# Reciprocal roots of the norms by Newton steps on VectorE, and the normalised input written by one VectorE product

## The chip, the core and the metric

The program runs on one core of a Trainium2 chip. The core has a matrix engine (TensorE, PE in the profile), a vector engine (VectorE, DVE), a scalar engine with function tables (ScalarE, ACT), a general engine (GpSimd, POOL) and a queue engine (SyncE, SP). Each works through its own list of instructions in order; an instruction starts when those before it on its engine have gone and the semaphores it waits for have been raised. The metric is the device time of one execution in microseconds (us): the median of several runs.

## What is computed

The input is one sequence of 2048 tokens with 256 features. Six sublayers follow one another. Each takes a layer norm of `x` first and adds its result to `x`:

```python
x = x + 0.5 * L0_ffn(layernorm(x))     # stage f0
x = x + L0_attn(layernorm(x))          # attention of layer 0
x = x + 0.5 * L0_ffn(layernorm(x))     # stage f1
x = x + 0.5 * L1_ffn(layernorm(x))     # stage f2
x = x + L1_attn(layernorm(x))          # attention of layer 1
x = x + 0.5 * L1_ffn(layernorm(x))     # stage f3

def _layernorm(x, axis=-1, eps=1e-05):
    m = jnp.mean(x, axis=axis, keepdims=True)
    v = jnp.var(x, axis=axis, keepdims=True)
    return (x - m) / jnp.sqrt(v + eps)

def rms_norm(x):
    inv = jax.lax.rsqrt(jnp.mean(xf * xf, axis=-1, keepdims=True) + eps)
    return (xf * inv).astype(x.dtype)
```

The feed-forward of layer 0 quantises its weights to three values per group of 64, computes `silu(gate) * up` over 1024 hidden features, takes an RMS norm of that, and projects back. The feed-forward of layer 1 keeps the two largest of each four hidden values. Attention has 16 heads of 16 features, a causal mask and, in layer 0, a linear position bias; layer 1 has a rotary embedding and biases.

## The kernel before

**Layout.** Everything is held with features on the partitions and tokens along the free axis. The 2048 tokens are cut into `NCH` = 4 chunks of `CH` = 512. `xs[c]` is the residual of chunk c, `xns[c]` its normalised form, each a tile of 128 partitions by 2 by 512 (`DC` = 2 halves of the features). The order on all four compute engines is the order of the program text (a manual schedule): what the generators below emit first runs first on its engine.

**A layer norm** is the generator `layernorm(c, name)`, lines 242 to 273, whose pieces are emitted between other work. GpSimd adds the two halves (line 249); TensorE multiplies by a matrix of 1/256 (line 253), which leaves the mean on every partition; VectorE subtracts it (line 255, tile `xc`); ScalarE squares (line 258); GpSimd adds the halves (line 260); TensorE takes the mean again (line 264). Then `root` (lines 202 to 209) transposes blocks of 32 by 32 on VectorE (line 206) so that the 512 variances stand as 128 by 16 values, and takes `Sqrt` on ScalarE (line 208). In the next piece `spread` (lines 211 to 219) takes the reciprocal on VectorE (line 213) and transposes back with a broadcast (line 215) into `sd`, 128 by 512. Last, GpSimd multiplies `xc` by `sd`, once for each half (line 269):

```python
nc.vector.transpose(tt.rearrange("p b s -> p (b s)"), ps)               # L206
nc.scalar.activation(r, tt[:, :, 0], AF.Sqrt, bias=eps, scale=scale)    # L208
nc.vector.reciprocal(r, r)                                              # L213
nc.gpsimd.tensor_tensor(xn[:, dc, :], xc[:, dc, :], sd, ALU.mult)       # L269
```

There are 24 layer norms. The RMS norm of layer 0's feed-forward uses the same `root` and `spread` in `tail0` (lines 349 to 371), 8 times, so `root` runs 32 times. The RMS result multiplies the projection on VectorE (line 369).

**ScalarE's tables.** `Silu` (line 317), `Exp` (lines 753 and 756) and `Sqrt` (line 208) need different function tables; the profile shows a table load ahead of the first instruction of another function, charged to that instruction's line.

**Feed-forward stages** (`feed_forwards`, lines 435 to 487) walk over chunks and, in each, over 8 blocks of 128 hidden features (f = 0 to 7). A step emits the matmuls of gate and up into one of two pairs of PSUM banks (line 306 in layer 0, 12 matmuls in bf16; line 281 in layer 1, 4 in f32), the `Silu` on ScalarE (line 317) and the product on VectorE (line 318). In layer 0 two more VectorE instructions split the product into bf16 parts (lines 334 and 329), and ScalarE and GpSimd build the sum of squares (lines 339, 340 and 336). In layer 1 `sparsify` (lines 385 to 421) compares and selects with VectorE (lines 394, 412 to 414, 418) and GpSimd (lines 405 to 409). After each step `pull()` (line 191) emits the next piece of up to two waiting layer norms, and the tail of the chunk before (`tail0` or `tail1`) emits one of its pieces. Stage f0 also quantises the weights on VectorE (lines 158 to 170). `split` (lines 234 to 240) divides `xns[c]` into bf16 parts on VectorE ahead of a chunk of layer 0.

**Attention** (`attention`, line 490) first finds the maxima of the scores: TensorE writes scores (lines 671 and 679) into one of three PSUM banks, VectorE reduces them (line 682). Transposed scores (lines 733, 741) then go through `Exp` on ScalarE (line 753) and into the product with the values (line 768). VectorE turns and divides the result (lines 789, 793, and on GpSimd 794). `prep_qk` makes the keys and queries of the next chunk (lines 536 to 588; in layer 1 GpSimd works at line 575).

**Where the layer norms fall.** By the times of line 206, 10 roots fall in stage f0 (three at its start, at 15, 61 and 63 us), 3 in the first attention (271, 289 and 382 us), 8 in f1, 5 in f2, 3 in the second attention (1240, 1256 and 1364 us) and 3 in f3 (two together at 1788 us).

Of the kernel before, what the change touches and what calls it, by code (L numbers as in the profile page):

```python
# [11 lines left out]

F32 = mybir.dt.float32
BF16 = mybir.dt.bfloat16
AF = mybir.ActivationFunctionType
ALU = mybir.AluOpType
AX = mybir.AxisListType
# [2 lines left out]
P = 128  # L20
S = 2048
E = 256
DC = E // P
H = 16
D = E // H
SLOT = 32
# [3 lines left out]
CH = 512  # L30
# [16 lines left out]
def macaron_kernel(ctx: ExitStack, tc: tile.TileContext, a, out):  # L47
    nc = tc.nc

    cpool = ctx.enter_context(tc.tile_pool(name="const", bufs=1))  # L50
# [10 lines left out]
    def ps_one(name):  # L61
        return ps3.tile([P, CH], F32, tag="one", name=name)
# [26 lines left out]
    make_identity(nc, ident)  # L89
    ident_b = cpool.tile([P, P], BF16, name="ident_b")  # L90
    nc.vector.tensor_copy(ident_b, ident)

    mask_qk = cpool.tile([P, P], BF16, name="mask_qk")
    mask_kq = cpool.tile([P, P], BF16, name="mask_kq")
    for mask, step, row in ((mask_qk, -1, 1), (mask_kq, 1, -1)):
# [5 lines left out]

    half_m = cpool.tile([P, P], BF16, name="half_m")
    nc.vector.memset(half_m, 0.0)
# [4 lines left out]
    nc.vector.memset(mean_m, 1.0 / E)  # L108
    ones_m = cpool.tile([P, P], F32, name="ones_m")
    nc.vector.memset(ones_m, 1.0)  # L110
    eps_ln = cpool.tile([P, 1], F32, name="eps_ln")
    nc.vector.memset(eps_ln, 1e-5)
    eps_rms = cpool.tile([P, 1], F32, name="eps_rms")
    nc.vector.memset(eps_rms, 4 * float(np.finfo(np.float32).eps))


    lpool = ctx.enter_context(tc.tile_pool(name="ln", bufs=1))
# [4 lines left out]
    w0pool = ffn0_scope.enter_context(tc.tile_pool(name="weights0", bufs=1, side="right"))  # L122
    wgu0 = w0pool.tile([P, DC, 2 * F], BF16, name="wgu0")
    wp0 = w0pool.tile([P, FC, E], BF16, name="wp0")
    raw_scope = ExitStack()
# [3 lines left out]
    def quantize(i):  # L129
# [19 lines left out]
        aw = qp.tile([P, 512], BF16, tag="aw", bufs=4, name=f"aw{i}")  # L149
        nc.scalar.activation(aw, raw, AF.Abs)  # L150
        sg = qp.tile([P, 512], BF16, tag="sg", bufs=4, name=f"sg{i}")
        nc.scalar.activation(sg, raw, AF.Sign)
        yield
# [48 lines left out]
    def root(ps, eps, scale, name):  # L202


        tt = lpool.tile([P, CH // SLOT, SLOT], F32, tag="tt", name=f"tt_{name}")
        nc.vector.transpose(tt.rearrange("p b s -> p (b s)"), ps)  # L206
        r = lpool.tile([P, CH // SLOT], F32, tag="r", bufs=3, name=f"r_{name}")
        nc.scalar.activation(r, tt[:, :, 0], AF.Sqrt, bias=eps, scale=scale)  # L208
        return r

    def spread(r, pool, bufs, name):

        nc.vector.reciprocal(r, r)  # L213
        sd = pool.tile([P, CH], F32, tag="sd", bufs=bufs, name=f"sd_{name}")
        nc.vector.transpose(
            sd.rearrange("p (b s) -> p b s", s=SLOT),
            r.unsqueeze(2).to_broadcast([P, CH // SLOT, SLOT]),
        )
        return sd
# [22 lines left out]
    def layernorm(c, name):  # L242

        pending[c] += 1

        def pieces():
            x, xn = xs[c], xns[c]
            s = lpool.tile([P, CH], F32, tag="s", bufs=2, name=f"s_{name}")
            nc.gpsimd.tensor_tensor(s, x[:, 0, :], x[:, 1, :], ALU.add)
            yield  # L250
            yield
            pm = ps_one(f"pm_{name}")
            nc.tensor.matmul(pm, lhsT=mean_m, rhs=s, start=True, stop=True)
            xc = lpool.tile([P, DC, CH], F32, tag="xc", bufs=2, name=f"xc_{name}")
            nc.vector.tensor_tensor(
                xc, x, pm.unsqueeze(1).to_broadcast([P, DC, CH]), ALU.subtract
            )
            nc.scalar.activation(xn, xc, AF.Square)
            v = lpool.tile([P, CH], F32, tag="s", bufs=2, name=f"v_{name}")
            nc.gpsimd.tensor_tensor(v, xn[:, 0, :], xn[:, 1, :], ALU.add)  # L260
            yield
            yield
            pv = ps_one(f"pv_{name}")
            nc.tensor.matmul(pv, lhsT=mean_m, rhs=v, start=True, stop=True)
            r = root(pv, eps_ln, 1.0, f"ln_{name}")
            yield
            sd = spread(r, lpool, 2, f"ln_{name}")
            for dc in range(DC):
                nc.gpsimd.tensor_tensor(xn[:, dc, :], xc[:, dc, :], sd, ALU.mult)  # L269
            pending[c] -= 1  # L270
            yield

        return pieces()


# [39 lines left out]
    def member(pg, to, hp, name):  # L315
        sl = hp.tile([P, CH], F32, tag="sl", bufs=2, name=f"sl_{name}")
        nc.scalar.activation(sl, pg[:, 0, :], AF.Silu)  # L317
        nc.vector.tensor_tensor(to, sl, pg[:, 1, :], ALU.mult)  # L318

    def steps0(c, xp, h, hp, own, name):  # L320
# [10 lines left out]
        for f in range(FC):  # L331
# [5 lines left out]
            else:  # L337
                sq = own.tile([P, CH], F32, tag="sq", bufs=2, name=f"sq_{name}_{f}")
                nc.scalar.activation(sq, h[:, f, :], AF.Square)  # L339
                nc.gpsimd.tensor_tensor(ss, ss, sq, ALU.add)  # L340
# [8 lines left out]
    def tail0(c, ss, parts, hp, name):  # L349

        yield
        pss = ps_one(f"pss_{name}")
        nc.tensor.matmul(pss, lhsT=ones_m, rhs=ss, start=True, stop=True)
        r = root(pss, eps_rms, 4.0 / F, f"rms_{name}")
        yield
        inv = spread(r, hp, 1, f"rms_{name}")
        for dc in range(DC):
            po = ps_one(f"po_{name}_{dc}")
            for f in range(FC):
                for part in range(3):  # L360
                    nc.tensor.matmul(
                        po,
                        lhsT=wp0[:, f, dc * P : (dc + 1) * P],
                        rhs=parts[f][part],
                        start=f == 0 and part == 0,
                        stop=f == FC - 1 and part == 2,
                    )
            y = hp.tile([P, CH], F32, tag="y", bufs=1, name=f"y_{name}_{dc}")
            nc.vector.tensor_tensor(y, po, inv, ALU.mult)
            nc.gpsimd.tensor_tensor(xs[c][:, dc, :], y, xs[c][:, dc, :], ALU.add)  # L370
            yield
# [793 lines left out]
```

## Time and profile before

| what | value |
|---|---|
| median of three runs | 1952.77 us (1952.13 to 1952.84) |
| the profiled execution, its own time | 1957.69 us |
| its span, first to last instruction | 1955.7 us |
| mean granted TensorE clock in it | 0.96 |
| table loads on ScalarE | 62, of 1283 ns each |
| GpSimd's products of line 269 | 48, 67.3 us in all |
| roots on ScalarE, line 208 | 32, of about 322 ns each |
| reciprocals on VectorE, line 213 | 32, of about 238 ns each |

The profile is taken from one execution, so durations and places below are read in its own span. Its lines name the engine, the line of the kernel, the tiles, a count, the busy time, the mean of one instruction and the idle time in front of it with what ended it. An engine that is idle costs nothing by itself; it matters where its work is the one that others wait for.

### The profile page before, as it was taken

To read this page: it belongs to the slowest core of one execution; us is meant where nothing else is said; L and a number is where in the kernel's file an instruction comes from. 1 tells how busy PE (TensorE), PEld (TensorE's weight loads), DVE (VectorE), ACT (ScalarE), POOL (GpSimd) and SP (SyncE) were. 2 spreads that over 40 slices of the span, in tenths; PEclk is the share of its full clock that TensorE was granted. 3 is DMA by queue.
4 is the path that set the end of the run, shared out by engine and by line. 5 is a ranking of instruction groups with operands and counts; after the bars stand their busy time and mean duration, and the time that the engine had idled before them with its cause. 6 is when DMAs were issued, how large, how long until landed. Compare 5 with 4: busy or idle time off the path is not lost. (4 is left out here: it accounts for less than half of the span.)

```text
span 1955.7 us, 26994 instructions
## 1 busy us (share of the span) xinstructions
PE 1761.4 (90%) x10684; PEld 726.5 (37%) x10684; DVE 1361.6 (70%) x2384; ACT 894.2 (46%) x1112; POOL 458.4 (23%) x418
## 2 busy tenths in 40 slices
PE   5699789999999999789999876898999999998997
PEld 1233344433433333333444333433333333333443
DVE  7866377787788883666575655868877888825664
ACT  4343254555555668334422312445555656673220
POOL 3455321101000000455453432211111000003422
PEclk9799899999999999989999986999999999999999
DMA  4000252213211000200000115222122110000000
GB/s 129 1 1 33 82 148 83 73 54 102 62 45 46 28 28 2 73 1 0 1 11 0 54 61 158 82 73 92 52 69 86 43 43 26 18 1 0 11 11 22
DMA packets 50510, 93.10 MB, mean 48 GB/s; under 512 B 5424, under 2 KB 33072, under 8 KB 50128
## 3 DMA queue, kind: packets, MB, share of 16 engines
q1 hardware_dynamic: 49296, 89.28, 14.8%
q10 hardware_dynamic: 1088, 2.10, 0.3%
q8 instruction: 84, 1.38, 0.3%
q14 instruction: 42, 0.34, 0.1%
HBM read 59.51 MB, written 27.26 MB: 44 GB/s over the span
## 5 line engine op out<-in xcount | busy, mean ns | idle before, releaser
L682 DVE TENSOR_REDUCE mx<-pq 128x1 f32<-128x512 f32 (+3 forms) x1280 | 708.6, 603 | 158.5 <-PE pq L679 91.2
L753 ACT ACTIVATE pT<-pst 128x1024 f32<-128x1024 f32 (+3 forms) x614 | 542.6, 896 | 334.9 <-PE pst L733 196.8
L671 PE MATMUL pq<-k,q 105*128 105x512 bf16 (+7 forms) x1280 | 378.8, 353 | 74.7 <-DVE mx L682 52.3
L733 PE MATMUL pst<-q,k 99*128 99x512 bf16 (+7 forms) x1280 | 357.7, 354 | 5.1 <-ACT pT L753 4.2
L768 PE MATMUL pav<-pT,va 128*32 128x256 f32 (+1 forms) x4608 | 352.4, 382 | 5.2 <-DVE yt L789 5.0
L281 PE MATMUL pg_f<-xn,wgu 128*128 128x512 f32 x512 | 229.8, 602 | 11.5 <-DVE hr_f L318 11.5
L794 POOL TENSOR_TENSOR zt<-yt,rd 128x64 f32<-128x64 f32 x128 | 38.4, 300 | 795.2 <-DVE rd L793 795.1
L733 PEld LDWEIGHTS <-k 105*128 105x128 bf16 (+1 forms) x1280 | 101.5, 98 | 254.1 <-issue 218.4
L317 ACT ACTIVATE sl_f<-pg_f 128x512 f32<-128x512 f32 x128 | 76.0, 594 | 251.8 <-PE pg_f L281 175.0
L671 PEld LDWEIGHTS <-q 105*128 105x128 bf16 (+1 forms) x1280 | 124.5, 100 | 148.0 <-issue 44.3
L306 PE MATMUL pg_f<-xn,wgu 128*128 128x512 bf16 x512 | 156.2, 413 | 19.5 <-DVE wgu L170 6.8
L768 PEld LDWEIGHTS pav<-pT,va 128*32 128x32 f32 x4608 | 93.8, 108 | 208.7 <-issue 174.8
L281 PEld LDWEIGHTS pg_f<-xn,wgu 128*128 128x128 f32 x512 | 98.6, 193 | 136.9 <-issue 121.0
L306 PEld LDWEIGHTS <-wgu 128*128 128x128 bf16 x768 | 77.7, 101 | 166.9 <-issue 74.7
L292 PE MATMUL po_f<-h_f,wd 128*128 128x512 f32 x256 | 116.3, 608 | 17.3 <-DVE h_f L418 17.3
L340 POOL TENSOR_TENSOR ss_f<-ss_f,sq_f 128x512 f32<-128x512 f32 x56 | 91.1, 1628 | 111.5 <-ACT sq_f L339 111.3
L679 PE MATMUL pq<-mask_qk,ident_b 128*128 128x128 bf16 x512 | 107.3, 227 | 0.0
L741 PE MATMUL pst<-mask_kq,ident_b 128*128 128x128 bf16 x512 | 103.1, 222 | 0.0
L306 PE MATMUL pg_f<-xm_f,wgu 128*128 128x512 bf16 x256 | 85.3, 416 | 14.0 <-DVE xm_f L238 14.0
L318 DVE TENSOR_TENSOR h_f<-sl_f,pg_f 128x512 f32<-128x512 f32 x64 | 43.6, 682 | 76.4 <-ACT sl_f L317 76.3
L789 DVE STREAM_TRANSPOSE yt<-pav 128x128 f32<-128x128 f32 x128 | 39.8, 311 | 76.7 <-PE pav L768 76.7
L394 DVE TENSOR_TENSOR ge_f<-h_f 128x1536 bf16<-128x1536 f32 (+2 forms) x48 | 67.6, 1437 | 28.0 <-ACT h_f L387 28.0
(132 smaller groups left out, 1802.5 us busy)
## 6 DMA issues: line engine op xcount, KB each, us to landing
k<-dk SPq DMA_DIRECT2D x80, 384.0 KB
dk<-p_k SPq DMA_DIRECT2D x48, 256.0 KB
dq<-p_q SPq DMA_DIRECT2D x48, 256.0 KB
q<-dq SPq DMA_DIRECT2D x32, 384.0 KB
x<-in_xT ACTq DMA_DIRECT2D x4, 512.0 KB
raw<-in_w_gu SPq DMA_DIRECT2D x8, 256.0 KB
wgu<-in_w_gu SPq DMA_DIRECT2D x1, 2048.0 KB
cs_k<-in_cos_sin SPq DMA_DIRECT2D x4, 512.0 KB
```

Of the source, the lines that this page charges most:

```text
L281: nc.tensor.matmul(pg[:, half, :], lhsT=wgu[:, dc, half * F + f * P : half * F + (f + 1) * P], rhs=xn[:, dc, :], start=dc == 0, stop=dc == ...
L292: nc.tensor.matmul(po, lhsT=w[:, f, dc * P : (dc + 1) * P], rhs=h[:, f, :], start=f == 0, stop=f == FC - 1,)
L306: nc.tensor.matmul(pg[:, half, :], lhsT=wgu0[:, dc, half * F + f * P : half * F + (f + 1) * P], rhs=xp[part][:, dc, :], start=part == 0 an ...
L317: nc.scalar.activation(sl, pg[:, 0, :], AF.Silu)
L340: nc.gpsimd.tensor_tensor(ss, ss, sq, ALU.add)
L671: nc.tensor.matmul(pq, lhsT=qs[n][0:rows, hh, t * P : (t + 1) * P], rhs=ks[n, kc][0:rows, hh, 0:w], start=True, stop=kc < c,)
L679: nc.tensor.matmul(pq[:, w - P : w], lhsT=ident_b, rhs=mask_qk, start=False, stop=True)
L682: nc.vector.tensor_reduce(mxs[n][:, t, hh, kc : kc + 1], pq, AX.X, ALU.max)
L733: nc.tensor.matmul(ps[i][:, lo:CH], lhsT=ks[n, kc][0:rows, hh, t * P : (t + 1) * P], rhs=qs[n][0:rows, hh, lo:CH], start=True, stop=kc < c,)
L741: nc.tensor.matmul(ps[i][:, lo : lo + P], lhsT=ident_b, rhs=mask_kq, start=False, stop=True)
L753: nc.scalar.activation(pT[:, :, lo:CH], pair[:, :, lo:CH], AF.Exp, scale=0.25)
L768: nc.tensor.matmul(acc[hh * SLOT : (hh + 1) * SLOT, a:b], lhsT=va[kc][:, t, v0 : v0 + SLOT], rhs=pTs[hh // 2][:, hh % 2, a:b], start=kb == ...
```

## The change

`root` no longer uses ScalarE. After the transpose of line 206, VectorE computes `v = scale * tt + eps`; shifts its bits right by one; subtracts that from a constant, as integers, which gives a first guess of the reciprocal root; and takes three Newton steps of three instructions each. These are 12 VectorE instructions on tiles of 128 by 16. `spread` loses its reciprocal. In `layernorm` the two GpSimd products of line 269 become one VectorE product over both halves, with `sd` broadcast. The two small tiles that held the epsilons become numbers.

```diff
     def root(ps, eps, scale, name):
         tt = lpool.tile([P, CH // SLOT, SLOT], F32, tag="tt", name=f"tt_{name}")
         nc.vector.transpose(tt.rearrange("p b s -> p (b s)"), ps)
-        r = lpool.tile([P, CH // SLOT], F32, tag="r", bufs=3, name=f"r_{name}")
-        nc.scalar.activation(r, tt[:, :, 0], AF.Sqrt, bias=eps, scale=scale)
+        shape = [P, CH // SLOT]
+        v = lpool.tile(shape, F32, tag="v", bufs=2, name=f"v_{name}")
+        nc.vector.tensor_scalar(v, tt[:, :, 0], scale, eps, ALU.mult, ALU.add)
+        e = lpool.tile(shape, F32, tag="e", bufs=2, name=f"e_{name}")
+        nc.vector.tensor_scalar(
+            e.bitcast(I32), v.bitcast(I32), 1, None, ALU.logical_shift_right
+        )
+        r = lpool.tile(shape, F32, tag="r", bufs=3, name=f"r_{name}")
+        nc.vector.tensor_scalar(
+            r.bitcast(I32), e.bitcast(I32), -1.0, float(0x5F3759DF), ALU.mult, ALU.add
+        )
+        for _ in range(3):
+            nc.vector.tensor_tensor(e, r, r, ALU.mult)
+            nc.vector.scalar_tensor_tensor(e, e, -0.5, v, ALU.mult, ALU.mult)
+            nc.vector.scalar_tensor_tensor(r, e, 1.5, r, ALU.add, ALU.mult)
         return r

     def spread(r, pool, bufs, name):
-        nc.vector.reciprocal(r, r)
         sd = pool.tile([P, CH], F32, tag="sd", bufs=bufs, name=f"sd_{name}")
...
             sd = spread(r, lpool, 2, f"ln_{name}")
-            for dc in range(DC):
-                nc.gpsimd.tensor_tensor(xn[:, dc, :], xc[:, dc, :], sd, ALU.mult)
+            nc.vector.tensor_tensor(xn, xc, sd.unsqueeze(1).to_broadcast([P, DC, CH]), ALU.mult)
             pending[c] -= 1
```

More of the change, by code (lines that the diff above doesn't have):

```diff
@@ L14 @@
 BF16 = mybir.dt.bfloat16
+I32 = mybir.dt.int32
 AF = mybir.ActivationFunctionType
@@ L110, in macaron_kernel @@
     nc.vector.memset(ones_m, 1.0)
[L111 to L114, printed above, removed]
+    eps_ln = 1e-5
+    eps_rms = 4 * float(np.finfo(np.float32).eps)
     lpool = ctx.enter_context(tc.tile_pool(name="ln", bufs=1))
```

## The prediction

> **What bounds the kernel now.** I read the page's busy shares first, then busy times by stage, then TensorE's waits, the rows of the touched lines, and last the timelines around each of the 32 roots.
>
> ```profile
> PE 1761.4 (90%) x10684; PEld 726.5 (37%) x10684; DVE 1361.6 (70%) x2384; ACT 894.2 (46%) x1112; POOL 458.4 (23%) x418
> 240.00:330.00 90.00, 77.10 (x593) 39.57 (x594) 69.99 (x175) 39.99 (x57) 17.38 (x25) 0.96 0.43 123
> 795.00:953.00 158.00, 139.25 (x552) 56.78 (x553) 109.91 (x134) 61.44 (x86) 88.13 (x57) 0.95 0.04 13
> ...
> PE pq L671 <- DVE mx L682: 52.3, 90, 8.1
> ```
>
> Columns of the two stretches: window, length, busy us of PE, weight loads, DVE, ACT, POOL, then granted clock and DMA. TensorE sets the pace, VectorE is second, and ScalarE, which the change relieves, is under half busy everywhere. In the first phase of an attention (240 to 330) VectorE is busy 78% and TensorE's largest named wait is for its maxima: there VectorE decides. In f1 (795 to 953) TensorE is busy 88% and VectorE 70%.
>
> **What is removed from ScalarE.**
>
> ```profile
> L208 ACT ACT_TABLE_LOAD x29 | 37.2, 1283 | 0.5
> L317 ACT ACT_TABLE_LOAD x24 | 30.8, 1283 | 35.6 <-PE pg_f L306 24.0 <-PE pg_f L281 11.0 <-issue 0.4
> L753 ACT ACT_TABLE_LOAD x8 | 10.3, 1283 | 0.1
> ```
>
> With one at line 150 these are 62 loads. Without Sqrt, Silu and Exp alternate only between stages: one load at the start, one for the first Silu, and four at the two entries and two exits of attention, 6 in all. So 56 loads go, 56 x 1.283 = 71.8 us, and 32 square roots of 0.32 us, 10.3 us. It is worth time only where a Silu or Exp that was ready stood behind it and someone waited.
>
> The rule I weighed: the Trainium skill, "ScalarE: Activation LUTs", section "What ACT_TABLE_LOAD costs", gives 1283 ns plus about 1380 ns of drain for a switch. By that an estimated 149 us of ScalarE would come free. The rows here show 1.28 us and the next ACTIVATE starting 0.01 us later (820.82 + 1.28, then 822.11), so no drain shows. The sum below is the same by either, because it prices waits and not ScalarE's busy time.
>
> **What is added to VectorE.**
>
> ```profile
> 257.32 0.18 DVE L689 TENSOR_REDUCE neg<-mx 128x16 f32<-128x16 f32 x1
> 257.53 0.39 DVE L694 TENSOR_TENSOR neg<-neg 128x16 f32<-128x16 f32 x2
> 281.88 1.35 DVE L694 TENSOR_TENSOR neg<-neg 128x16 f32<-128x16 f32 x2
> 281.94 1.27 POOL L260 TENSOR_TENSOR v_after_f<-xn 128x512 f32<-128x512 f32 x1 [1.81 <-ACT xn L258]
> ...
> L213 DVE RECIPROCAL r_ln_f<-r_ln_f 128x16 f32<-128x16 f32 x16 | 3.8, 238 | 0.0
> L577 DVE TENSOR_TENSOR dn_k<-dn_k,sw_k x4: 1197/1212/1224, 1104.7 to 1450.2; 128x1024 f32<-128x1024 f32 x4
> ```
>
> A chain of VectorE instructions on 128 x 16, each needing the one before, advances 0.21 us at the first (257.32 to 257.53) and 0.39 / 2 = 0.195 us in the pair. I take 0.20 us: 12 x 0.20 = 2.4 us for a root, less the reciprocal (0.28 us from 116.58, its start, to 116.86, the next start), so +2.12 us. No row shows a bit shift or an integer product; their bounds are 0.18 us (line 689) and 0.24 us (line 213), which give 1.88 to 2.6. The new product reads two SBUF tiles of 128 x 1024: 1.21 us (line 577), no less, since nothing of that size and kind is shorter. It takes the place of two GpSimd products (67.3 us in all).
>
> The same instruction beside GpSimd: the pair at 281.88 took 1.35 us instead of 0.39 while GpSimd ran 281.94 to 283.21. So a VectorE instruction with two SBUF inputs waits out a GpSimd one, +0.96 us. The change meets this on both sides: nine of the twelve small instructions have two SBUF inputs, and 48 GpSimd products go. The second side I added up where line 269 overlaps such VectorE instructions: 1.7 us at 20, 3.2 at 70, 1.8 at 118, 3.2 at 826, 1.8 at 868, 2.0 at 1007 and 3.5 at 1794, about 17 us. VectorE in all: 32 x 2.12 + 24 x 1.21 - 17 = +80 us.
>
> The rule behind that row: the Trainium skill, "SBUF — State Buffer", section "Who interferes with whom", says that the second to issue blocks until the first has finished, whatever its size. By it a root that meets a queue of four GpSimd instructions of 1.27 us, as in `sparsify`, could lose an estimated 5 us, which would add some 8 us to the sum at f2 and f3. The row's one meeting cost 0.96 us.
>
> **What of it is on the path.** Most is not. After 90 us in f0, and in f1 to f3, TensorE runs two pairs of banks ahead. The old root also held up the product of line 318, by a load, the root and a load (2.9 us); the new one holds it by 2.4 us on VectorE. Example: at 133.58 line 206 runs, the product follows at 136.59, behind the late Silu; with the change it follows at 133.58 + 0.71 + 2.4 = 136.7. Equal, and nothing waits; if TensorE's lead were gone, such a root would cost its 2.12 us. I went through the other roots one by one.
>
> Start: the first norm's chain gains 2.12 + 1.21 and loses 1.7 of blocking: +1.6. At 61 to 72 us quantising keeps VectorE full. Two roots follow each other (+4.8); VectorE idled 1.45 us there, since the second transpose waited for the first root; two reciprocals go (0.56), two products come (2.42), 3.2 of blocking goes: +2.0.
>
> Gains at GpSimd:
>
> ```profile
> 117.76 2.94 POOL L269 TENSOR_TENSOR xn<-xc_f,sd_ln_f 128x512 f32<-128x512 f32 x2
> 120.66 1.71 POOL L249 TENSOR_TENSOR s_after_f<-x 128x512 f32<-128x512 f32 x1
> ...
> 122.42 1.45 PE L253 MATMUL pm_after_f<-s_after_f,mean_m 128*128 128x512 f32 x2 [4.21 <-POOL s_after_f L249]
> ```
>
> The sum of line 249 stood behind the two products; it can start 2.9 us earlier. The same happens at 873.34 (4.21 us). Together -5.8, because the wait's other 1.3 us stay.
>
> Start of f1, 818 to 835: two roots in a row. From the first transpose I lay out VectorE's list again: the products of lines 318 come 2.4 us later, then two products come (2.42), two reciprocals and 3.2 of blocking go, and line 238 ends about 0.7 us later: +0.7. The waits 1011 and 1801 go the same way:
>
> ```profile
> 1790.82 1.28 ACT L317 ACT_TABLE_LOAD   x1 [0.83 <-PE pg_f L281]
> 1792.75 0.69 DVE L318 TENSOR_TENSOR hr_f<-sl_f,pg_f 128x512 f32<-128x512 f32 x1 [1.29 <-ACT sl_f L317]
> ...
> 1801.46 8.80 PE L281 MATMUL pg_f<-xn,wgu 128*128 128x512 f32 x16 [3.85 <-DVE hr_f L318]
> ```
>
> At 1801 two roots (+4.8) and two products (+2.42) meet 1.68 of idle time filled (0.39 and the 1.29 above), 0.5 of reciprocals and 3.5 of blocking: +1.5. At 1011: 2.4 + 1.21 - 0.28 - 0.23 - 2.0 = +1.1. At 1054 line 418 ends 2.1 us later, 0.8 us after TensorE wants it for line 292: +0.8. For new meetings of small instructions with GpSimd's queue in f2 and f3: +1.0.
>
> Attention: in its first phase VectorE is nearly unbroken, and the chain of waits runs through it:
>
> ```profile
> 1256.35 0.72 DVE tt_ln_after_f L206
> ...
> 1261.97 0.71 DVE sd_ln_after_f L215
> ```
>
> What is queued behind the root there are the maxima, for which TensorE waits. Two roots and products cost 2 x 3.33 = 6.7 us; a third later (382, 1364), where VectorE idles some 0.4 us per unit, costs perhaps 1.5; and Exp, no longer behind a load, gives back the 0.93 us that line 733 waited at 292.37 and 1243.39. So +7.3 for each attention, +14.6. If all of VectorE's idle time there took it in, this would be nothing.
>
> The sum: 1.6 + 2.0 - 5.8 + 0.7 + 1.5 + 1.1 + 0.8 + 1.0 + 14.6 = +17.5 us. The profiled execution took 1957.7 us (its span 1955.7), 4.9 above the median; so it would take 1975.2, and the median of the runs 1952.8 + 17.5 = 1970.3 us.
>
> **Rivals.** *VectorE's gaps take it in (no change).* For it: TensorE busy 90%, and f0 after 90 us and f1 show VectorE idle a quarter of the time. Against it: the chain through lines 206 and 215 at 1256. With attention at +2 instead of 14.6 the time is 1957.7; with the small step at 0.18, 32 x 0.24 us less on VectorE, a few of them on the path, 1955.
>
> *The table switch was the path (faster).* Mechanism: where a Silu stands behind load, root and load, TensorE loses; ScalarE free, these waits end. Price: 2.73 at 823.48, 3.85 at 1801.46, 1.8 at 1011.73, and 4.21 twice at GpSimd, 16.8 us, with attention unchanged: 1936. It decides if the Newton chain takes well under the 2.9 us that it replaces, also where two follow each other, that is if a small step takes about 0.1 us. Against it: no instruction of 128 x 16 in the page is below 0.18.
>
> *GpSimd blocks the chain (much slower).* Each of the 16 roots in f1, f2 and f3 loses 0.96 us or more, several times where `sparsify` queues; with half of it on the path and attention as forecast, +17.5 + 16 = 1986. For it: line 694 at 281.88. Against: GpSimd is busy 23%, less without line 269.
>
> That the change doesn't do what it says (a load of another table stays for Square or Sign) is excluded by the timeline: Square at 823.52 and Silu at 824.06 follow each other without a load.
>
> **How the numbers follow.** Forecast, 1958 to 1980: 0.55. Blocking, above 1980: 0.15. No change, within 0.2% (about what a measurement of this kernel can tell from no change, 1948.9 to 1956.7): 0.12. Faster: 0.18. Slower 0.70. The range takes in the small step's bounds (32 x -0.24 to +0.48 us, half on the path: -4 to +8), attention from 0 to 20, and reaches into the faster case and over the blocking one: 1945 to 1988. The likeliest case's own range is 1958 to 1980.
>
> **What would show it.** Table loads 6; line 208 gone; 12 rows of 128 x 16 for each root at about 0.20 us; VectorE busy near 1440 us, ScalarE near 812, GpSimd near 391. Steps right: TensorE's wait for line 682 up by 10 us or more, the waits at 122 and 873 down to about 1.3 us. Wrong: the rows at 0.1 us or at 0.4; or attention's stretch as long as before, which would leave about +3.

## The result and the profile after

The changed kernel takes 1980.24 us (median of 4 runs, 1976.49 to 1983.73) against 1952.80 us before (1952.13 to 1955.01): +27.4 us, ratio 1.0135 with a 95% interval of 1.0117 to 1.0153. A second set of runs (`changed_again` below) gave 1.0145 (1.0126 to 1.0163). The forecast was 1970.3, with a range of 1945 to 1988, a likeliest range of 1958 to 1980, and slower at 0.70.

The changed kernel's page, busy times of the engines, then its ScalarE groups by line, the table loads (busy us, mean ns | idle before):

```profile
PE 1758.9 (89%) x10659; PEld 726.0 (37%) x10684; DVE 1441.2 (73%) x2758; ACT 812.8 (41%) x1024; POOL 390.4 (20%) x370
```

```profile
L329 ACT ACT_TABLE_LOAD x3 | 3.8, 1283 | 20.7 <-PE pg_f L318 11.1 <-PE pg_f L293 9.3 <-issue 0.4
L765 ACT ACT_TABLE_LOAD x2 | 2.6, 1283 | 0.0
L149 ACT ACT_TABLE_LOAD x1 | 1.3, 1283 | 1.2 <-PEq L1167 1.2
```

Six loads are left of 62, and ScalarE's busy time fell from 894.2 to 812.8 us. VectorE's rose from 1361.6 to 1441.2. TensorE does the same work (1758.9 against 1761.4), so what was lost is TensorE's waiting. Its longest waits, us in all, times, longest (changed kernel):

```profile
PE pq L683 <- DVE mx L694: 68.4, 99, 8.2
PE pg_f L318 <- DVE xm_f L251: 19.2, 8, 2.9
PE po_f L304 <- DVE h_f L430: 17.3, 2, 10.2
PE pg_f L293 <- DVE hr_f L330: 16.0, 5, 5.9
```

The first was 52.3 us before: 16.1 us more, in the attentions, where scores wait for the maxima.

Where along the span the time went can be read without any attribution. TensorE issues the same 10,684 weight loads in the same order in both kernels, so the k-th start of one trace can be set against the k-th of the other. The lag of the changed kernel at the ends of the stages, for two profiled executions of it (1978.78 us, and 1984.41 us from the run `changed_again` below), against the one of before (1957.69 us):

| us added in | forecast | first profile | second profile |
|---|---|---|---|
| start and f0 (to 240) | +0.7 | +3.9 | +3.9 |
| attention 0 (to 795) | +7.3 | +7.2 | +8.4 |
| f1 (to 953) | -2.2 | +0.2 | +2.6 |
| f2 (to 1160) | +1.9 | +0.7 | +0.6 |
| attention 1 (to 1765) | +7.3 | +5.9 | +6.8 |
| f3 (to the last weight load) | +1.5 | +3.5 | +4.7 |
| all | +17.5 (with 1.0 of new blocking in f2 and f3) | +21.3 | +26.9 |

The forecast column is the prediction's own terms put in their stages. Two stages carry most of the surprise: f0 and f1, where 5.8 us of gain were counted and 1.3 us came.

### The profile page after: what moved, and what is told of

The parts are those of the page before. It is cut to its first block, busy times and chain, and to the rows that moved or that the text cites. A ratio compares the mean times of both kernels' runs of the same rounds, so it can differ in the third digit from the quotient of the medians.

```text
span 1977.0 us, 27207 instructions
## 1 busy us (share of the span) xinstructions
PE 1758.9 (89%) x10659; PEld 726.0 (37%) x10684; DVE 1441.2 (73%) x2758; ACT 812.8 (41%) x1024; POOL 390.4 (20%) x370
## 5 line engine op out<-in xcount | busy, mean ns | idle before, releaser
L351 ACT ACTIVATE sq_f<-h_f 128x512 f32<-128x512 f32 x56 | 35.3, 630 | 121.7 <-DVE h_f L330 121.7
```

## The experiments

Eleven runs followed. Each time stands beside before's median of the same call (1953.63, 1954.28 or 1954.60 us); the interval is of the ratio.

| run | us | against before | ratio (95%) |
|---|---|---|---|
| newton_gps | 1978.43 | +24.8 | 1.0123 (1.0103 to 1.0142) |
| sqrt_vec | 1953.00 | -0.6 | 1.0000 (0.9989 to 1.0011) |
| one_step | 1963.00 | +9.4 | 1.0044 (1.0029 to 1.0059) |
| ffn_only | 1961.66 | +8.0 | 1.0046 (1.0034 to 1.0059) |
| changed_again | 1982.64 | +28.4 | 1.0145 (1.0126 to 1.0163) |
| gps_steps | 1984.81 | +30.5 | 1.0161 (1.0142 to 1.0180) |
| vec_ffn | 1949.04 | -5.2 | 0.9980 (0.9967 to 0.9994) |
| spread_steps | 1969.09 | +14.8 | 1.0079 (1.0063 to 1.0095) |
| loads_back | 1982.12 | +27.5 | 1.0140 (1.0120 to 1.0160) |
| spread_all | 1998.33 | +43.7 | 1.0219 (1.0198 to 1.0240) |
| mix | 1954.93 | +0.3 | 0.9995 (0.9982 to 1.0009) |

### Which half of the change costs: newton_gps and sqrt_vec

newton_gps keeps the chain and gives the product back to GpSimd:

```diff
-            nc.vector.tensor_tensor(xn, xc, sd.unsqueeze(1).to_broadcast([P, DC, CH]), ALU.mult)
+            for dc in range(DC):
+                nc.gpsimd.tensor_tensor(xn[:, dc, :], xc[:, dc, :], sd, ALU.mult)
```

> The Newton chain on VectorE stays, the normalised input goes back to two GpSimd products. Theory (the loss is the chain's VectorE time at the places where TensorE waits for VectorE, and the move of the product is about even): +16 to +22 us against before; the two waits for GpSimd's sum at 122 and 873 us of the span are back at 4 us; an attention loses 4 to 5 us instead of 7. Rival (the VectorE product is the main cost): not over +9 us.

sqrt_vec keeps the VectorE product and puts the square root and the reciprocal of before back in `root` and `spread`:

```diff
-        v = lpool.tile(shape, F32, tag="v", bufs=2, name=f"v_{name}")
...
-            nc.vector.scalar_tensor_tensor(r, e, 1.5, r, ALU.add, ALU.mult)
+        r = lpool.tile([P, CH // SLOT], F32, tag="r", bufs=3, name=f"r_{name}")
+        nc.scalar.activation(r, tt[:, :, 0], AF.Sqrt, bias=eps, scale=scale)
...
+        nc.vector.reciprocal(r, r)
```

> Square root on ScalarE and reciprocal as before, the normalised input in one VectorE product. Theory: -4 to +4 us against before: an attention loses 2.7 to 3.5 us (two or three products of 1.2 to 1.35 us), and the two waits for GpSimd's sum end with nothing given back behind them, -3 us each, since the chain isn't in VectorE's queue there. Rival (the product is the main cost): +15 us or more.

The chain costs +24.8 us alone, a little over the theory's 16 to 22; the product alone is even. Their sum, +24.2, misses the whole's +27 to +28 by no more than the intervals allow. The rival, that the product is the main cost, falls. In newton_gps the two waits for GpSimd's sum are back, at 3.15 and 3.14 us where 4 were expected. The attentions missed their numbers: newton_gps adds +8.4 and +4.0 us there in its profile (4 to 5 each expected), sqrt_vec -0.4 and +0.7 (2.7 to 3.5 each expected).

And one sentence of the theory for sqrt_vec was wrong: "nothing given back behind them". TensorE's timeline at the second of the two places (start, duration, instruction [wait <- for whom]), before:

```profile
873.34 1.43 PE L253 MATMUL pm_f<-s_f,mean_m 128*128 128x512 f32 x2 [4.21 <-POOL s_f L249]
...
877.73 0.61 PE L306 MATMUL pg_f<-xm_f,wgu 128*128 128x512 bf16 x2
```

TensorE's and VectorE's in sqrt_vec:

```profile
865.50 1.12 PE L255 MATMUL pm_f<-s_f,mean_m 128*128 128x512 f32 x2 [1.83 <-POOL s_f L251]
...
869.56 1.21 DVE L257 TENSOR_TENSOR xc_f<-x,pm_f 128x1024 f32<-128x1024 f32 x1
870.69 1.22 DVE L240 TENSOR_TENSOR xm_f<-xn 128x1024 f32<-128x1024 f32 x1
...
871.96 0.61 PE L307 MATMUL pg_f<-xm_f,wgu 128*128 128x512 bf16 x2 [2.18 <-DVE xm_f L240]
```

and in the changed kernel:

```profile
881.58 1.12 PE L266 MATMUL pm_f<-s_f,mean_m 128*128 128x512 f32 x2 [0.76 <-POOL s_f L262]
...
888.05 0.73 PE L318 MATMUL pg_f<-xm_f,wgu 128*128 128x512 bf16 x2 [2.19 <-DVE xm_f L251]
```

The wait for GpSimd's sum shrank from 4.21 us to 1.83 and 0.76, and 6.5 us later TensorE waits 2.2 us for the next input's split (line 240 there, 251 in the changed kernel), which it did not before. The new wait is the same with and without the chain, so the chain is not its cause. Between the reciprocal and the end of the split VectorE has 10.3 us of work before (867.49 to 877.79) and 9.9 us in sqrt_vec (862.03 to 871.91): the old GpSimd wait had stood in front of VectorE's queue, which was nearly as late (the split ended at 877.79 before, and TensorE took it up at once).

### How much the chain's length counts: one_step

```diff
-        for _ in range(3):
+        for _ in range(1):
```

> Leaves out two of the three Newton steps, so the roots are rough; six of the twelve small VectorE instructions of a root go, 32 x 6 x 0.21 = 40 us of VectorE. Theory (half of the 32 roots stand where TensorE waits for VectorE): 16 x 1.25 = 20 us under the changed kernel, near 1960 us. Rival (VectorE's share of busy time counts, wherever it is): half of the added time goes, so half of the loss, near 1967 us. Rival (code size, the clock or other fixed costs): no change.

With one step of three the roots are rough, and the kernel takes 1963.0 us, 17.2 us under the changed kernel's 1980.24. That lies between the two estimates of 20 and 13 and nearer the first; 17.2 of the 40 us taken from VectorE reached the end, 43%. A fixed cost is out.

### Where it costs: ffn_only

```diff
+    as_before = ('ln_after_f0_2', 'ln_after_f0_3', 'ln_f1_0', 'ln_after_f2_2', 'ln_after_f2_3', 'ln_f3_0')
...
+        if name in as_before:
+            r = lpool.tile([P, CH // SLOT], F32, tag="r", bufs=3, name=f"r_{name}")
+            nc.scalar.activation(r, tt[:, :, 0], AF.Sqrt, bias=eps_t, scale=scale)
+            return r
```

The reciprocal and the GpSimd products are back for the same names.

> The six norms whose roots run inside the attentions are done as before (square root, reciprocal, two GpSimd products), the other 26 roots as changed. Theory: the two attentions' loss goes, 7.2 + 6.2 = 13.4 us under the changed kernel, near 1967 us, and the attentions are as long as before. Rival (loss in proportion to VectorE's added time): 6 x (2.2 + 1.35) = 21 of 80 us go, a quarter of the loss, near 1973 us.

It takes 1961.66 us: six norms of 24, each with its root and its product, carry 18.6 of the 27.4 us. Theory asked for 13.4, the proportional rival for 7. Its attentions add -2.9 and +0.1 us to before's instead of +7.2 and +5.9. So a root costs where TensorE waits for VectorE, and an average over the span says nothing of it.

### Were the table loads on the path: loads_back

```diff
+        unused = lpool.tile([P, CH // SLOT], F32, tag="unused", bufs=2, name=f"u_{name}")
+        nc.scalar.activation(unused, tt[:, :, 0], AF.Sqrt, bias=eps_t, scale=scale)
```

> The changed kernel, with a square root on ScalarE added at each root whose result nobody reads, so the table loads and square roots are back (near 62 loads, about 82 us of ScalarE) while nothing waits for them but what stands behind them on ScalarE. Theory (the loads were worth little, since ScalarE is under half busy): 0 to +5 us against the changed kernel, +26 to +32 against before. Rival (the loads' removal gave 8 us or more, hidden in the sum by VectorE's loss): +35 us or more against before.

The page and the ScalarE groups of loads_back:

```profile
PE 1762.9 (89%) x10684; PEld 726.5 (37%) x10684; DVE 1444.2 (73%) x2759; ACT 894.7 (45%) x1112; POOL 389.9 (20%) x370
```

```profile
L210 ACT ACT_TABLE_LOAD x29 | 37.2, 1283 | 0.5
L333 ACT ACT_TABLE_LOAD x24 | 30.8, 1283 | 34.1 <-PE pg_f L322 23.4 <-PE pg_f L297 10.1 <-issue 0.4
```

ScalarE is back at 894.7 us with its 62 loads, and the time is 1982.12 us, +27.5 against before where the changed kernel had +27.4 and +28.4. So in the changed kernel the 82 us less of ScalarE are worth nothing. That alone does not say what the loads cost in the kernel of before, since here VectorE's chain runs beside them and may hide them. one_step answers that: its six small instructions take about 1.26 us (an estimate, 6 x 0.21) in place of the 2.9 us of load, root and load, no load is left, and it still runs 9.4 us slower than before.

The Trainium skill, "ScalarE: Activation LUTs", section "What ACT_TABLE_LOAD costs", counts some 1380 ns of drain on top of each load; whatever of it there is, this run had it 56 times more than the changed kernel and was no slower.

### Another engine for the steps: gps_steps

```diff
-            nc.vector.tensor_tensor(e, r, r, ALU.mult)
-            nc.vector.scalar_tensor_tensor(e, e, -0.5, v, ALU.mult, ALU.mult)
-            nc.vector.scalar_tensor_tensor(r, e, 1.5, r, ALU.add, ALU.mult)
+            nc.gpsimd.tensor_tensor(e, r, r, ALU.mult)
+            nc.gpsimd.tensor_tensor(e, e, v, ALU.mult)
+            nc.gpsimd.tensor_scalar(e, e, -0.5, 1.5, ALU.mult, ALU.add)
+            nc.gpsimd.tensor_tensor(r, r, e, ALU.mult)
```

> The three Newton steps run on GpSimd, in four instructions a step instead of three (it is given no instruction with two operations on two tensors); start value and product stay on VectorE. VectorE loses 32 x 9 x 0.21 = 60 us of work against the changed kernel, ScalarE keeps its 6 table loads. Theory (VectorE's time decides, table loads were hidden): -4 to +6 us against before, not faster than the kernel with square roots and the VectorE product by more than 3 us. Rival (the table loads were on the path and VectorE's chain hid the gain): -8 us or more against before. Rival (the chain's length counts, on whichever engine): GpSimd's 12 instructions take 3 us or more, so +15 us or more.

+30.5 us: the theory as it was put, VectorE's time alone, falls, and the rival that asked for +15 us or more, the chain's length on whichever engine, is right. VectorE is busy 1398.1 us, 43 less than in the changed kernel, and the kernel is no faster. The timelines of gps_steps at the start of f1, and TensorE's in f3:

```profile
831.48 1.22 DVE L281 TENSOR_TENSOR xn<-xc_f,sd_ln_f 128x1024 f32<-128x1024 f32 x1
831.55 1.24 POOL L222 TENSOR_TENSOR r_ln_f<-r_ln_f,e_ln_f 128x16 f32<-128x16 f32 x1
...
835.20 0.71 DVE L228 STREAM_TRANSPOSE sd_ln_f<-r_ln_f 128x512 f32<-128x512 f32 x1 [2.50 <-POOL r_ln_f L222]
...
838.12 1.01 PE L318 MATMUL pg_f<-xn,wgu 128*128 128x512 bf16 x2 [7.12 <-DVE h_f L330]
...
1826.95 3.78 PE L293 MATMUL pg_f<-xn,wgu 128*128 128x512 f32 x4 [9.67 <-DVE hr_f L330]
```

A GpSimd chain advances about 0.30 us an instruction (826.32, 826.61, 826.92, 827.22): twelve take 3.5 us at the least and 4.1 to 5.1 us in 21 of the 32 chains. Two roots here run one after the other. VectorE's transpose waits 2.50 us for the second one, and the product of line 330 queued behind it keeps TensorE waiting for 7.12 us. In f1 this wait stands in place of others, and the stage adds only +0.4 us to before's. The same queue costs more later: f2 adds +6.4 and f3 +7.2 (changed kernel: +0.7 and +3.5), the attentions +6.4 and +6.6, f0 nothing. An engine that is idle inside its queue is as late as one that is busy: what counts is how long the chain holds up what stands behind it.

### One piece or several: spread_steps and spread_all

spread_steps changes only the six norms in the attentions. Their steps and their product are issued in successive turns of the background work:

```diff
-            r = root(pv, eps_ln, 1.0, f"ln_{name}")
+            if name in in_attention:
+                r, e, v = root(pv, eps_ln, 1.0, f"ln_{name}", 0)
+                for _ in range(3):
+                    yield
+                    newton(r, e, v)
+            else:
+                r = root(pv, eps_ln, 1.0, f"ln_{name}")
             yield
             sd = spread(r, lpool, 2, f"ln_{name}")
+            if name in in_attention:
+                yield
```

> The changed kernel, but in the six norms inside the attentions the three Newton steps and the product are issued one at a time, in successive turns of the background work, instead of a chain in one piece. Theory (VectorE has no slack in that phase, so its added time counts wherever it stands): within 4 us of the changed kernel, +21 to +28 us against before. Rival (the chain in one piece holds up the maxima, and VectorE's idle time between them would take it in pieces): 8 to 14 us under the changed kernel.

1969.09 us, 13.5 us under changed_again in the same call: the rival is right. The changed kernel's timeline in attention 1 shows one root in one piece:

```profile
1250.61 0.72 DVE L206 STREAM_TRANSPOSE tt_ln_after_f<-pv_after_f 128x512 f32<-128x512 f32 x1 [0.25 <-PE pv_after_f L277]
...
1254.12 0.18 DVE L222 SCALAR_TENSOR_TENSOR r_ln_after_f<-e_ln_after_f,r_ln_after_f 128x16 f32<-128x16 f32 x1
1254.21 1.94 DVE L694 TENSOR_REDUCE mx<-pq 128x1 f32<-128x384 f32 x4
1254.82 0.32 PE L683 MATMUL pq<-k,q 99*128 99x384 bf16 x1 [2.68 <-DVE mx L694]
```

From 1250.61 to 1254.21 VectorE takes no maximum, and TensorE waits 2.68 us for a free bank of scores. In spread_steps the same stretch reads:

```profile
1248.72 0.18 DVE L217 TENSOR_SCALAR r_ln_after_f<-e_ln_after_f 128x16 int32<-128x16 int32 x1
1248.81 1.95 DVE L711 TENSOR_REDUCE mx<-pq 128x1 f32<-128x384 f32 x4
...
1251.63 0.17 DVE L232 SCALAR_TENSOR_TENSOR r_ln_after_f<-e_ln_after_f,r_ln_after_f 128x16 f32<-128x16 f32 x1
1251.72 1.41 DVE L711 TENSOR_REDUCE mx<-pq 128x1 f32<-128x256 f32 x4
```

Each step stands between two groups of maxima and holds them up by 0.6 us. The two attentions add +5.0 and -0.4 us to before's, where the changed kernel adds +7.2 to +8.4 and +5.9 to +6.8, although VectorE does the same work (1441.0 us). How much of the relief belongs to the steps and how much to the product, which moved too, was not tried apart.

spread_all does the same in all layer norms but the first, with four buffers instead of two or three for the small tiles (`if name != "f0_0"` in place of `if name in in_attention`).

> Every layer norm but the first issues its Newton steps and its product one at a time in successive turns of the background work, in the feed-forward stages too; the roots inside the output projections stay in one piece. With the attentions alone in pieces the kernel took +15 us. Theory (a chain in one piece is what costs, everywhere): +8 to +12 us against before. Rival (outside the attentions VectorE's total or the norm's own length decides): +15 us or more, as the norms become ready up to four turns later.

+43.7 us, and the theory falls outside the attentions. TensorE's waits in spread_all:

```profile
PE pg_f L334 <- DVE xn L297: 26.6, 3, 11.5
...
PE pg_f L309 <- DVE xn L297: 10.4, 1, 10.4
```

TensorE waits 37.0 us for the normalised input itself, in four places (changed kernel: 3.6 us for the same product). In the attentions the normalised input is early even in pieces: in spread_steps the six products end 22 to 395 us before TensorE reads them. In a feed-forward stage the next chunk starts with it, and four turns more are a delay.

### A faster version: vec_ffn and mix

vec_ffn is sqrt_vec with the product on VectorE in the norms outside the attentions and on GpSimd in the six inside:

```diff
-            nc.vector.tensor_tensor(xn, xc, sd.unsqueeze(1).to_broadcast([P, DC, CH]), ALU.mult)
+            if name in in_attention:
+                for dc in range(DC):
+                    nc.gpsimd.tensor_tensor(xn[:, dc, :], xc[:, dc, :], sd, ALU.mult)
+            else:
+                nc.vector.tensor_tensor(xn, xc, sd.unsqueeze(1).to_broadcast([P, DC, CH]), ALU.mult)
```

> Square roots on ScalarE everywhere; the product on VectorE in the 18 norms outside the attentions and on GpSimd in the six inside. Theory: the VectorE product costs 2 to 3 us in each attention and gains a little outside, so -3 to -6 us against before: faster than both kernels. Rival (the product is even everywhere): 0.

1949.04 us, ratio 0.9980 (0.9967 to 0.9994): the lowest median of all, 31 us under the changed kernel, and under the one of before by 5.2 us in the medians (1.2 to 6.4 by the interval). That it beats sqrt_vec (0.9989 to 1.0011) is not shown, as the intervals overlap. TensorE's wait for the maxima in sqrt_vec and in vec_ffn:

```profile
PE pq L672 <- DVE mx L683: 56.6, 97, 8.1
PE pq L678 <- DVE mx L689: 51.4, 91, 8.1
```

In vec_ffn it is no more than before's 52.3 us. mix adds Newton roots in pieces inside the attentions to it:

> Outside the attentions square root, reciprocal and the VectorE product; inside them Newton steps, one a turn, and two GpSimd products. Against before: -5 us from the part outside (as measured with square roots everywhere), and the six Newton roots inside add 6 x 2.2 us of VectorE in pieces, of which the idle time takes most, while 6 x 1.28 us x 2 of table loads there go. Theory (in pieces most of it is hidden): -6 to 0 us. Rival (half of VectorE's added time still counts): 0 to +4 us.

+0.3 us (0.9982 to 1.0009): between the theory's -6 to 0 and the rival's 0 to +4, so it decides neither. Its median is 5.6 us over vec_ffn's by what each shows against before, but the intervals overlap, so that it is slower is not shown. A gain from the steps in pieces, and from the table loads that they replace, does not show.

### The spread between executions: changed_again

> The changed kernel once more, for a second trace and more times beside the others of this call: +24 to +29 us against before. Theory (the profiled execution of before held some 4 us more of half-clock stretches than usual, in attention at 328, 502 and 1236 us): a second profile shows the same steps along TensorE's instructions, within 1.7 us each.

+28.4 us, as expected. The second trace is 5.6 us longer than the first; the steps along TensorE's instructions are in the same places, with stages up to 2.4 us apart (1.7 expected). The theory of the half-clock stretches holds only in part. Windows of before's profile (length, busy us of PE, PEld, DVE, ACT, POOL, then granted clock), the first two at places that the expectation names:

```profile
327.90:331.30 3.40, 3.34 (x4) 1.32 (x5) 1.20 (x3) 0.00 (x0) 0.20 (x1) 0.50 0.00 0
502.00:505.40 3.40, 3.40 (x14) 0.79 (x13) 2.93 (x5) 1.60 (x2) 0.00 (x0) 0.50 0.00 0
```

and the second one's place in the changed kernel:

```profile
513.20:516.60 3.40, 3.06 (x19) 1.04 (x18) 3.40 (x7) 2.05 (x2) 0.00 (x0) 1.00 0.01 3
```

TensorE passes 14 matmuls there at half clock and 19 at full clock, and the lag of the changed kernel shrinks by 1.25 us at that point. Summed over the clock's rows, half clock was granted for 157 us before, 154 in the first profile of the changed kernel and 169 in the second. That accounts for most of what separates the two profiles of the changed kernel: the stages in which the second had more (attention 0, f1 and f3, 3.4 to 6.9 us each) are longer by 1.2 to 2.4 us each. That before's profile had more of it than usual in the attentions does not hold: it had 71 us there, the other twelve profiles 62 to 82.

## Why the prediction was right, and where it was not

**The costs.** VectorE was forecast near 1440 us busy, ScalarE near 812, GpSimd near 391, six table loads; measured were 1441.2, 812.8, 390.4 and six. One Newton step's instructions in the changed kernel, by VectorE group:

```profile
L221 DVE SCALAR_TENSOR_TENSOR e_ln_f<-e_ln_f,v_ln_f 128x16 f32<-128x16 f32 x48 | 8.4, 175 | 1.7
L220 DVE TENSOR_TENSOR e_ln_f<-r_ln_f 128x16 f32<-128x16 f32 x48 | 8.4, 175 | 1.6
L222 DVE SCALAR_TENSOR_TENSOR r_ln_f<-e_ln_f,r_ln_f 128x16 f32<-128x16 f32 x48 | 8.4, 175 | 1.7
```

0.175 us busy and some 0.035 idle is 0.21 us each, and an unhindered chain ends 2.51 us after its transpose where 2.4 were said. The product took 1.31 to 1.52 us on the average instead of 1.21: its shortest took 1.22 us, and those beside GpSimd's other work up to 2.2.

**The attentions**, +14.6 forecast, gave +13.1 and +15.2 in the two profiles and about 18.6 by the medians of ffn_only: right in place and somewhat small in size. The reason given, that VectorE "is nearly unbroken" there, is only half right. spread_steps leaves VectorE's work as it is and takes most of the loss away, so there was idle time to take it; the chain in one piece could not use it, because the maxima queue behind it in order and TensorE has only three banks for scores.

**The step that failed** is "Gains at GpSimd": "Together -5.8, because the wait's other 1.3 us stay." The waits did fall, to 0.77 and 0.76 us at 122 and 873, but the lag fell by 3.6 us at each place and rose again within 8 us, at the split's wait: -0.5 us net at the first (4.2 to 3.7), -0.8 at the second (11.9 to 11.1). The working stopped at the wait that was removed and never asked what TensorE would wait for next; it was VectorE, already as late. This step alone is 4.5 us of the 9.9 by which the forecast fell short.

**Terms mis-sized.** At 1801 the sum had +1.5; f3 lost 3.5 us and more. The changed kernel's timeline there:

```profile
1806.42 1.15 POOL L418 TENSOR_TENSOR ct_f<-ct_f,ge_f 128x512 bf16<-128x512 bf16 x1
...
1806.57 1.03 DVE L211 TENSOR_SCALAR e_ln_f<-v_ln_f 128x16 int32<-128x16 int32 x1
...
1815.90 2.00 DVE L281 TENSOR_TENSOR xn<-xc_f,sd_ln_f 128x1024 f32<-128x1024 f32 x1
```

Line 211 waits out GpSimd's `ct`, 1.03 us for 0.17, and the product took 2.00 us for 1.21: the credit of 3.5 us for blocking relieved was partly spent on new blocking. Up to the product of line 330 ahead of the two norms' products VectorE had lost 3.9 us where the sum's terms give 3.1 (4.8 less 1.68); from there to the next one it regained 0.35 us where they give 1.6. At 1054 the 0.8 us did not appear; at 1005 to 1011 it was +1.5 to +1.7 for +1.1. The start was +1.8 for +1.6 and the roots at 61 to 72 us +2.4 for +2.0, nearly as worked out. f1's start was +0.7 in both profiles, as forecast; the second one's 2.4 us more in f1 came ahead of it, where that profile has a stretch of half clock (809.95, 3.41 us) that the first has not. The attentions by the medians were 4.0 us more than forecast. With the 4.5 above and the 2.0 of f3 that is about the whole shortfall; it is a rough sum, since it takes medians and traces together.

**The rivals.** That the table switch was the path is refuted by loads_back and one_step together. That VectorE's gaps take it in was wrong for this order of work and nearly right for another, spread_steps. That GpSimd blocks the chain had its mechanism confirmed: in the first profile one small instruction took 0.99 to 1.19 us in five of the 32 chains, three of them among the 16 of f1, f2 and f3, of which the rival wanted all: too seldom to decide. The measured 1980.24 lies 0.2 us above the likeliest case's range, in the part that the prediction gave to this rival at 0.15. The gains that did not come put it there more than blocking did: all 32 chains together lost 6.5 us by it, and only a part of that stood on TensorE's path.

## What to carry to other kernels

Before counting a removed wait as gain, look for the instruction that TensorE needs next and ask when its engine would have had it ready; a wait on one engine often stands in front of an equal one on another. Work added to an engine with idle time is free only if it is issued in pieces no longer than the slack behind it, and only where its result is not itself due; the same chains and products cost about 18 us or 5 us in the attentions by their place in the queue alone. What it is worth to take load from an engine that is under half busy is best read from a run with the load put back; here it was nothing.

## What the runs showed of the hardware

Blocking goes both ways: a GpSimd instruction on 128x16 that takes 0.22 us took 1.24 us when it began 0.07 us after a VectorE product with two SBUF inputs (831.48 in gps_steps). The Trainium skill, "SBUF — State Buffer", section "Who interferes with whom", says that the second to issue waits for the first whatever its size; the 1.24 us beside a 1.22 us product agree. The other way round, line 211 took 1.03 us for 0.17 beside a GpSimd instruction (1806.57), though it reads one tensor: the blocking is not limited to VectorE instructions with two SBUF inputs, as the prediction took it to be. The instruction on 128x16 with a shift on int32 costs the same 0.175 us as a float product; nothing in the trace of before had shown that. And TensorE's clock falls to half for stretches of 3.4 us and multiples of it, 143 to 176 us of a span in the thirteen profiles, not at the same places in every execution. One such stretch at 502 us moved the lag by 1.25 us; by an estimate it can be 1.7 us, half of 3.4. A difference of a few us between two single traces can therefore be the clock's.
